# Cross-attention with a scan on one core: folded maxima, statistics on ScalarE, halved projections

## The chip, the cores and the metric

The kernel runs on one NeuronCore of a Trainium2 chip. The core has five engines with instruction queues of their own: TensorE (PE: matmuls and transposes, results into PSUM; its weight loads stand in the profile as PEld), VectorE (DVE), ScalarE (ACT), GpSimd (POOL) and SyncE (SP, which here issues nearly all DMAs). The metric is the time of one execution on the device, in microseconds. Before the change it was 2542.23 us, the median of three runs (2541.93 to 2543.82).

## The reference

One layer of a sequence model in fp32. Cut to what is computed:

```
x      = builder_state                                  # 4096 x 512
base   = layernorm(ctx, g1, beta1)                      # 3202 x 512
h      = x + mha(layernorm(x, g1, beta1), base)         # 8 heads of 64
U      = (layernorm(h, g2, beta2) @ W_in.T + b_in) @ Bmat   # 4096 x 64
s_t    = silu(s_(t-1) @ A.T) + U_t                      # a scan over 4096 steps
out    = h + states @ Cmat + mean(ctxb) @ W_prog.T + b_prog

mha:   scores = q @ k.T / 8;  softmax over 3202 keys;  @ v;  @ W_o.T + b_o
```

The softmax is over all 3202 keys of a query, with the row's maximum taken off first.

## The kernel before

**Preparation.** The context is read in 26 chunks of 124 or 123 keys (`keys`, `key0`, lines 44 to 49). Each is normalized (statistics on DVE, factors on POOL, scaling on ACT), transposed on PE and projected to values (`pv`, L505) and, four chunks at a time, to keys (`pk`, L531), which go out to DRAM (`vd`, `kd`). A side generator (`side`, L355) folds gains and biases into the weights between the chunks, and at its end `first_queries` (L284) normalizes the first 512 query rows and makes all four query tiles of block 0 (`heads`, L265: 4 head pairs, each two halves of 256 queries by four 128x256 matmuls into the PSUM tile `pq`, then one ACT eviction to `q`).

**Main part.** The work is 64 units: 8 query blocks of 512 by 4 head pairs by 2 halves of 256 queries. A unit takes 13 steps, one for each pair of key chunks. For step c:

- `scores` (PE, L576): four matmuls into `s`, a PSUM tile of [keys, head a, chunk b, 256 queries]; two such buffers.
- `keep` (ACT, L589): a copy of `s` to SBUF (`p`).
- `top` (DVE, `running`, L597): the running maximum over the steps, still one value per key row, head, chunk of the pair and query: 1024 elements.

After the 13th `top`, `spread` (PE, L605) transposes `top` in 128-query tiles: two tiles `tt` of four 124x124 blocks each; `maximum` (DVE, L615) reduces each to one value per head and query; `everywhere` (PE, L625) transposes these back over the key rows into `mb`. Then, again for each step: `subtract` (DVE, L633), `weights` (ACT, exp, L643), `add` (POOL, L651, the running sum `acc`) and `product` (PE, L660, into `po`). `finish` (L708) turns the sum into reciprocals (`both` POOL, `turn` and `back` PE, `inverse` DVE, `wide` ACT, `scale` DVE).

Beside the units run two kinds of other work, cut into pieces. `queries` (L788) prepares block Q+1: per 128 rows a load, the three pieces of `norm_pieces` (L767: `stats` on DVE, `factors` on POOL, `scaled` on ACT), a transposition and its copy; then four `heads` of 16 matmul records each, as one piece. `project` (L831) finishes block Q: per 128 rows a load, `row` (POOL), `outs` (PE, `pa`, four 128x512 matmuls in one piece), `x1` (DVE), `norm_pieces`, `mod` (POOL), a store, a transposition and copy, `inputs` (PE, `pu`) and `kept` (DVE, L900), which writes the scan's inputs `u`.

**Order.** Nothing in this part is in program order as written. `Plan` (L52) holds pieces with an engine, a cost in ns, what they come after, a due time, and the ring buffers they take and give back. `Plan.order` (L77) goes through a modelled time, picks for each free engine the ready piece with the smallest due time whose buffers fit, and the pieces are emitted in that order; each engine then executes its own in that order. On PE, entering a group of another kind costs `START`, staying in it `AGAIN`, and up to two pieces of the same kind are pulled together.

**End.** The last unit's row sums are partly made on PE (`last_sums`, L668), and the scan over the sequence follows, in blocks, with the output rows.

Of the kernel before, what the change touches and what calls it, by code (L numbers as in the profile page):

```python
# [20 lines left out]
P = 128  # L21
# [22 lines left out]
def keys(c):  # L44
    return CK if c < GC else CK - 1


def key0(c):
    return c * (CK - 1) + min(c, GC)


class Plan:  # L52
# [8 lines left out]
    START, AGAIN = 215, 90  # L61
# [6 lines left out]
    def add(self, name, engine, cost, run, after=(), due=0, take=(), give=(), kind=None):  # L68
        assert name not in self.pieces, name
        self.pieces[name] = dict(  # L70
# [6 lines left out]
    def order(self):  # L77
# [21 lines left out]
        while len(out) < len(pieces):  # L99
            for e in self.LATE:  # L100
# [3 lines left out]
                for p in ready[e]:  # L104
                    if fits(p):
                        more = p["kind"] and p["kind"] == last and run < 2
                        key = p["due"] - (6000 if more and e == "PE" else 0), p["at"]
                        if best is None or key < best[0]:
                            best = key, p
# [33 lines left out]
def xattn_ssm_kernel(  # L143
# [49 lines left out]
    bu = const.tile([P, 1], F32, name="bu")  # L193

# [70 lines left out]
    def heads(Q, hp, xns):  # L265

        pq = ps_m.tile([P, 512], F32, tag="m", name=f"pq_{Q}_{hp}")
        for half in range(2):
            for i in range(NC):
# [12 lines left out]
        qt[Q, hp] = t  # L282

    def first_queries(x0):  # L284
# [16 lines left out]
        for hp in range(NC):  # L301
            for _ in heads(0, hp, xns):
                yield
            yield

# [49 lines left out]
    def side():  # L355
# [62 lines left out]
        for k in (0, NS):  # L418
            nc.vector.tensor_copy(bu[k : k + NS], pb[:NS, 0:1])

# [170 lines left out]
    def running(w, c):  # L591

        n, s = keys(2 * c), w["ps"][c]
        before = w["s"][0] if c == 1 else w["top"]
        if c == 1:
            w["top"] = accp.tile([CK, 2, 2, QU], F32, tag="top", name=f"top_{w['name']}")
        nc.vector.tensor_tensor(w["top"][:n], s[:n], before[:n], ALU.max)  # L597

    def spread(w, t):

        tp = ps_m.tile([P, 2, 2, CK], F32, tag="m", name=f"tt_{w['name']}_{t}")
        w["tt", t] = tp
        for a in range(2):
            for b in range(2):
                nc.tensor.transpose(  # L605
                    tp[:, a, b, :],
                    w["top"][:, a, b, t * P : (t + 1) * P],
                    ident[:CK, :CK],
                )

    def maximum(w, t):

        if t == 0:
            w["m"] = small.tile([P, 2, 2], F32, tag="m", name=f"m_{w['name']}")
        nc.vector.tensor_reduce(  # L615
            w["m"][:, t, :], w["tt", t].rearrange("p a b k -> p a (b k)"), AX.X, ALU.max
        )
# [149 lines left out]
    def norm_pieces(plan, k, get, d, after, name, give):  # L767
# [3 lines left out]
        def stats_():  # L771
            v["mv"] = stats(get(), P, name)

        def factors_():
            v["fs"] = factors(v["mv"], P, name)

        def scaled_():
            v["xh"] = scaled(get(), v["fs"], P, name)
# [681 lines left out]
```

## Time and profile before

| | us |
|---|---|
| median of three runs | 2542.23 |
| the profiled execution | 2546.95 |
| its span, first to last instruction | 2545.1 |
| first scores matmul at | 262.67 |
| first `mb` (maxima of unit 0 spread) at | 291.42 |
| last `mb` at | 2441.61 |

The costliest groups of the page, with the number of instructions, the busy time and the mean of one:

| line, engine | what | count | busy us | mean ns |
|---|---|---|---|---|
| L651 POOL | `add` | 698 (and 64 first ones) | 1651.1 (152.2) | 2366 (2378) |
| L633 DVE | `subtract` | 832 | 997.9 | 1210 |
| L576 PE | `scores` | 6656 | 907.5 | 398 |
| L660 PE | `product` | 6656 | 880.1 | 391 |
| L643 ACT | `weights` | 832 | 876.4 | 1059 |
| L597 DVE | `top` | 704 (and 64 first ones) | 856.1 (78.0) | 1216 (1219) |
| L589 ACT | `keep` | 832 | 826.8 | 1006 |
| L270 PE | `heads` | 512 | 118.7 | 385 |
| L848 PE | `outs` | 240 | 110.4 | 603 |
| L615 DVE | `maximum` | 128 | 84.6 | 668 |
| L605 PE | `spread` | 512 | 73.8 | 278 |

Smaller rows of the answer by line: `bn_stats` L212 62 times on query and row tiles, 0.69 us each, `bn_aggr` L214 0.18; the POOL factors 0.22, 0.56 and 0.27 (L221, L223, L225); the scaling L233 on ACT 0.81; `kept` L900 on DVE 0.44; `x1` L858 on DVE 0.68; the PSUM copy `xn` on ACT 0.59.

How to read it: the busy time of a group is the union of its instructions' spans, and successive ones overlap, so counts times means are more than the busy time. A fp32 matmul stands as two records. What a piece costs its engine is best read from its start to the start of the next. An idle time is put down to what ended it last.

### The profile page before, as it was taken

The numbers are of one execution on the slowest core, as the hardware profiler recorded it, in microseconds if no ns is written. First come the engines' busy times: TensorE is split into PE (matmuls) and PEld (weight loads), VectorE is DVE, ScalarE is ACT, GpSimd is POOL, SyncE is SP. The second block draws the span as 40 slices with busy tenths as digits, with TensorE's granted clock in tenths as the row PEclk, the third lists the DMA queues.
The fourth block names the chain that finished last, engine by engine and source line by source line (L and its number), as shares of the span: only waits on it lengthen the run. The fifth ranks groups of instructions, "written<-read, shape, count | busy, mean of one in ns | idle before, by whom it ended". The sixth has DMA issues, their size and how long they took to land.

```text
span 2545.1 us, 44356 instructions
## 1 busy us (share of the span) xinstructions
PE 2439.3 (96%) x16648; PEld 1435.7 (56%) x16648; DVE 2128.5 (84%) x2322; ACT 1838.7 (72%) x2111; POOL 2071.1 (81%) x1195
## 2 busy tenths in 40 slices
PE   7989799999999999999999999999999999999997
PEld 3445455655565556655565556555665556555543
DVE  2220699999989999899989998999989998999974
ACT  2222688787878788787878887878878787878752
POOL 1010299899988999899989999899989998999973
PEclk9999999999999999999999999999999999999998
DMA  3422322112211221122211221222112221233364
GB/s 126 141 87 68 90 61 61 50 42 69 72 46 56 71 69 55 46 65 75 67 51 43 65 88 34 60 68 68 53 49 65 71 67 52 79 115 113 105 168 142
DMA packets 178035, 189.22 MB, mean 74 GB/s; under 512 B 14252, under 2 KB 151256, under 8 KB 177818
## 3 DMA queue, kind: packets, MB, share of 16 engines
q1 hardware_dynamic: 173270, 178.67, 23.5%
q10 hardware_dynamic: 4548, 7.67, 0.9%
q8 instruction: 134, 2.20, 0.4%
q14 instruction: 83, 0.68, 0.1%
HBM read 156.40 MB, written 29.89 MB: 73 GB/s over the span
## 4 chain that ended last, share of the span: by engine, by line
PE 52%; DVE 23%; issue 9%; ACT 6%; POOL 5%; DMA 3%; SPq 1%; ACTq 0%; POOLq 0%; DVEq 0%
PE s L576 16%; DVE top L597 14%; PE po L660 13%; DVE p L633 6%; POOL acc L651 5%; PE pq L270 4%; PE pa L848 4%; ACT p L589 3%; PE pv L505 3%; PE pk L531 3%; PE tt L605 2%; ACT p L643 2%; DMA x<-in_x_dram 2%; PE mb L625 1%; PE pu L894 1%
## 5 line engine op out<-in xcount | busy, mean ns | idle before, releaser
L651 POOL TENSOR_TENSOR acc<-p,acc 123x1024 f32<-123x1024 f32 x698 | 1651.1, 2366 | 65.3 <-ACT p L643 24.4
L633 DVE TENSOR_TENSOR p<-p,mb 123x1024 f32<-123x1024 f32 (+1 forms) x832 | 997.9, 1210 | 4.0 <-PE mb L625 3.8
L643 ACT ACTIVATE p<-p 123x1024 f32<-123x1024 f32 (+1 forms) x832 | 876.4, 1059 | 171.9 <-DVE p L633 169.2
L589 ACT COPY p<-s 123x1024 f32<-123x1024 f32 (+1 forms) x832 | 826.8, 1006 | 222.0 <-PE s L576 200.2
L576 PE MATMUL s<-q,k 64*123 64x256 f32 (+1 forms) x6656 | 907.5, 398 | 43.9 <-DVE top L597 31.9
L597 DVE TENSOR_TENSOR top<-s,top 123x1024 f32<-123x1024 f32 x704 | 856.1, 1216 | 53.1 <-ACT p L589 50.8
L660 PE MATMUL po<-p,v 123*64 123x256 f32 (+1 forms) x6656 | 880.1, 391 | 3.8 <-ACT p L643 2.7
L576 PEld LDWEIGHTS s<-q,k 64*123 64x123 f32 (+1 forms) x6656 | 574.3, 182 | 336.9 <-DVE top L597 152.1
L660 PEld LDWEIGHTS po<-p,v 123*64 123x64 f32 (+1 forms) x6656 | 416.7, 136 | 364.8 <-issue 154.8
L651 POOL TENSOR_TENSOR acc<-p,p 124x1024 f32<-124x1024 f32 x64 | 152.2, 2378 | 128.6 <-DMA k<-kd 77.6
L597 DVE TENSOR_TENSOR top<-s,p 124x1024 f32<-124x1024 f32 x64 | 78.0, 1219 | 60.3 <-DMA k<-kd 37.5
L221 POOL TENSOR_SCALAR ve_c<-mv_c 123x1 f32<-123x1 f32 (+1 forms) x26 | 5.8, 225 | 145.7 <-DVE mv_c L214 115.2
L270 PE MATMUL pq<-xn,wq 128*128 128x256 f32 x512 | 118.7, 385 | 0.0
L475 DVE COPY ct<-tp_c 128x492 f32<-128x492 f32 (+1 forms) x13 | 8.7, 671 | 127.2 <-PE tp_c L248 127.2
L848 PE MATMUL pa<-wo,o 128*128 128x512 f32 x240 | 110.4, 603 | 0.0
L270 PEld LDWEIGHTS pq<-xn,wq 128*128 128x128 f32 x512 | 94.8, 190 | 23.2 <-issue 9.4
L615 DVE TENSOR_REDUCE m<-tt 128x2 f32<-128x496 f32 x128 | 84.6, 668 | 22.0 <-PE tt L605 21.3
L539 ACT ACTIVATE ks<-pk,bias 128x492 f32<-128x492 f32 (+2 forms) x28 | 18.0, 642 | 111.5 <-PE pk L531 56.9
L505 PE MATMUL pv<-wv,ct 128*123 128x512 f32 (+1 forms) x208 | 97.2, 612 | 0.0
L531 PE MATMUL pk<-ct,wk 128*128 128x492 f32 (+2 forms) x224 | 89.2, 550 | 0.0
L716 POOL TENSOR_TENSOR both<-acc 124x512 f32<-124x512 f32 x63 | 80.8, 1283 | 2.4
L605 PE MATMUL tt<-ident,top 124*128 124x124 f32 x512 | 73.8, 278 | 9.0 <-DVE top L597 7.2
(182 smaller groups left out, 1331.9 us busy)
## 6 DMA issues: line engine op xcount, KB each, us to landing
k<-kd SPq DMA_DIRECT2D x396, 123.0 KB
v<-vd SPq DMA_DIRECT2D x396, 123.0 KB
k<-kd SPq DMA_DIRECT2D x72, 124.0 KB
v<-vd SPq DMA_DIRECT2D x72, 124.0 KB
xr<-in_x_dram SPq DMA_DIRECT2D x32, 256.0 KB
x1d<-xr SPq DMA_DIRECT2D x32, 256.0 KB
x<-in_x_dram SPq DMA_DIRECT2D x28, 256.0 KB
cx<-in_ctx_dram SPq DMA_DIRECT2D x22, 246.0 KB
```

Of the source, the lines that this page charges most:

```text
L270: nc.tensor.matmul(pq[:, half * QU : (half + 1) * QU], wq[:, i, hp * P : (hp + 1) * P], xns[half][:, i, :], start=(i == 0), stop=(i == NC ...
L505: nc.tensor.matmul(pv[:n, :H], ct[:, i, o : o + n], wv[:, i, :], start=(i == 0), stop=(i == NC - 1),)
L531: nc.tensor.matmul(pk[:, :n_g], wk[:, i, hp * P : (hp + 1) * P], ct[:, i, :n_g], start=(i == 0), stop=(i == NC - 1),)
L576: nc.tensor.matmul(s[:n, a, b, :], kts[(*w["at"][:2], c)][r, b * n : (b + 1) * n], q[r], start=True, stop=True,)
L589: nc.scalar.copy(t[:n], w["ps"][c][:n])
L597: nc.vector.tensor_tensor(w["top"][:n], s[:n], before[:n], ALU.max)
L605: nc.tensor.transpose(tp[:, a, b, :], w["top"][:, a, b, t * P : (t + 1) * P], ident[:CK, :CK],)
L633: nc.vector.tensor_tensor(t[:n], t[:n], w["mb"][:n].unsqueeze(2).to_broadcast([n, 2, 2, QU]), ALU.subtract,)
L643: nc.scalar.activation(t[:n], t[:n], AF.Exp)
L651: nc.gpsimd.tensor_tensor(w["acc"][:n], t[:n], before[:n], ALU.add)
L660: nc.tensor.matmul(w["po"][a * HD : (a + 1) * HD, 0, :], vts[(*w["at"][:2], c)][:n, b, a * HD : (a + 1) * HD], t[:n, a, b, :], start=(c == ...
L848: nc.tensor.matmul(v["pa"], o_t[Q, c, t // 2][:, t % 2 * P : (t % 2 + 1) * P], wo[:, c, :], start=(c == 0), stop=(c == NC - 1),)
```

## The change

Six edits. (1) The key chunks are cut so that the last pair has 124 rows. At the last step of a unit DVE folds the two chunks of the pair together: `s0 = max(s0, top0)` in PSUM, `top1 = max(s1, top1)`, `top0 = max(s0, top1)`, each of 512 elements, in place of one maximum of 1024. `spread` transposes only `top0`: four blocks into one tile, and `maximum` is one reduction. (2) In `norm_pieces` the two DVE statistics give way to two ACT passes with accumulated output, the negated mean (`mean`) and the sum of squares about it (`spread`); POOL makes the factors from them. (3) `kept` moves from DVE to ACT, with a doubled bias `bu2`. (4) `heads` and `outs` become two pieces each. (5) `first_queries` makes only head pair 0; pairs 1 to 3 become pieces of the plan, due 4 steps apart from step 4 on, and the first units wait for their own `q`. (6) The planner gets other entry costs, a penalty for a lone piece of a kind (`ALONE`) and a shift of due times by the sort of piece (`SHIFT`).

```diff
@@ keys, key0
 def keys(c):
-    return CK if c < GC else CK - 1
+    return {0: CK, 1: CK, 2: CK - 2, NDC - 1: CK}.get(c // 2, CK - 1)
 def key0(c):
-    return c * (CK - 1) + min(c, GC)
+    return sum(keys(k) for k in range(c))
@@ class Plan
-    START, AGAIN = 215, 90
+    START, AGAIN = 200, 65
+    RUN = 2
+    ALONE = dict(scores=600, product=2600)
+    SHIFT = {
+        "back": -2600, "both": -1300, "everywhere": -2600, "heads": 2000, "heads2": -5200,
+        "maximum": 18900, "output": -5200, "product": 1300, "query.spread": -5800,
+        "query.turn": 1200, "row.mean": 2000, "row.mod": 7800, "row.row": 1300, "row.spread": -600,
+        "row.turn": 2600, "spread": -2000, "turn": -1900, "weights": 1300,
+    }
...
+        due += self.SHIFT.get(sort, 0)
...
-                        more = p["kind"] and p["kind"] == last and run < 2
-                        key = p["due"] - (6000 if more and e == "PE" else 0), p["at"]
+                        due = p["due"]
+                        if p["kind"]:
+                            if p["kind"] == last and run < self.RUN:
+                                due -= 6000
+                            elif p["kind"] != last or run >= self.RUN:
+                                others = [o for o in ready[e] if o["kind"] == p["kind"] and o is not p]
+                                if not any(fits(dict(take=o["take"] + p["take"])) for o in others):
+                                    due += self.ALONE[p["kind"]]
@@ heads, first_queries
         for half in range(2):
+            if half:
+                yield
             for i in range(NC):
...
-        for hp in range(NC):
-            for _ in heads(0, hp, xns):
-                yield
+        first_xns.extend(xns)
+        pieces = heads(0, 0, xns)
+        next(pieces)
+        for _ in pieces:
             yield
+        yield
@@ side
             nc.vector.tensor_copy(bu[k : k + NS], pb[:NS, 0:1])
+            nc.vector.tensor_scalar(bu2[k : k + NS], pb[:NS, 0:1], 2.0, None, ALU.mult)
@@ running
+        if c == NDC - 1:
+            top0, top1 = (before[:n, :, b, :] for b in range(2))
+            nc.vector.tensor_tensor(s[:n, :, 0, :], s[:n, :, 0, :], top0, ALU.max)
+            nc.vector.tensor_tensor(top1, s[:n, :, 1, :], top1, ALU.max)
+            nc.vector.tensor_tensor(top0, s[:n, :, 0, :], top1, ALU.max)
+            return
@@ spread, maximum
-    def spread(w, t):
-        tp = ps_m.tile([P, 2, 2, CK], F32, tag="m", name=f"tt_{w['name']}_{t}")
-        w["tt", t] = tp
-        for a in range(2):
-            for b in range(2):
+    def spread(w):
+        tp = ps_m.tile([P, 2, 2, CK], F32, tag="m", name=f"tt_{w['name']}")
+        w["tt"] = tp
+        for t in range(2):
+            for a in range(2):
                 nc.tensor.transpose(
-                    tp[:, a, b, :],
-                    w["top"][:, a, b, t * P : (t + 1) * P],
-                    ident[:CK, :CK],
+                    tp[:, t, a, :], w["top"][:, a, 0, t * P : (t + 1) * P], ident[:CK, :CK]
                 )
-    def maximum(w, t):
-        if t == 0:
-            w["m"] = small.tile([P, 2, 2], F32, tag="m", name=f"m_{w['name']}")
-        nc.vector.tensor_reduce(
-            w["m"][:, t, :], w["tt", t].rearrange("p a b k -> p a (b k)"), AX.X, ALU.max
-        )
+    def maximum(w):
+        w["m"] = small.tile([P, 2, 2], F32, tag="m", name=f"m_{w['name']}")
+        nc.vector.tensor_reduce(w["m"], w["tt"], AX.X, ALU.max)
@@ norm_pieces
-        def stats_():
-            v["mv"] = stats(get(), P, name)
+        def mean_():
+            xh = v["xh"] = ln.tile([P, H], F32, tag="xh", name=f"xh_{name}")
+            v["nm"] = ln.tile([P, 1], F32, tag="nm", name=f"nm_{name}")
+            nc.scalar.activation(
+                xh, get(), AF.Copy, scale=-1.0 / H, accum_out=v["nm"]
+            )
+        def spread_():
+            v["sq"] = ln.tile([P, 1], F32, tag="sq", name=f"sq_{name}")
+            nc.scalar.activation(
+                v["xh"], get(), AF.Square, bias=v["nm"], accum_out=v["sq"]
+            )
         def factors_():
-            v["fs"] = factors(v["mv"], P, name)
+            rstd = v["rstd"] = ln.tile([P, 1], F32, tag="rstd", name=f"rstd_{name}")
+            nc.gpsimd.tensor_scalar(rstd, v["sq"], 1.0 / H, EPS, ALU.mult, ALU.add)
+            nc.gpsimd.tensor_tensor(rstd, rstd, neg_half, ALU.pow)
+            nc.gpsimd.tensor_tensor(v["nm"], v["nm"], rstd, ALU.mult)
...
-        plan.add((*k, "stats"), "DVE", 860, stats_, after, d, ["st", "mv"],
-                 [("st", (*k, "stats")), give])
...
+        plan.add((*k, "mean"), "ACT", 820, mean_, after, d, ["nm", "xh"])
+        plan.add((*k, "spread"), "ACT", 820, spread_, [(*k, "mean")], d + 1000, ["sq"])
@@ queries, head_pieces
+    def head_pieces(plan, Q, hps, xns, copied, d, apart, xn_):
+        for hp in hps:
...
+            plan.add(("heads", Q, hp), "PE", 1850, head, copied, d, ["m", "q"], xn_)
+            plan.add(("heads2", Q, hp), "PE", 1850, lambda v=v: next(v["heads"]),
+                     [("heads", Q, hp)], d + 1, [], xn_)
...
@@ project
-            def outs(v=v, r=r, t=t):
-                v["pa"] = ps_m.tile([P, H], F32, tag="m", name=f"pa_{r}")
-                for c in range(NC):
+            def outs(part, v=v, r=r, t=t):
+                if part == 0:
+                    v["pa"] = ps_m.tile([P, H], F32, tag="m", name=f"pa_{r}")
+                for c in (2 * part, 2 * part + 1):
...
+            plan.add((*k, "outs2"), "PE", 1850, partial(outs, 1), [(*k, "outs")], d + 1, [], o_)
...
             def kept(v=v, hs=hs, c0=c0):
-                nc.vector.tensor_scalar(
+                nc.scalar.activation(
                     u[hs, :, c0 : c0 + P // L].rearrange("s j c -> s c j"),
                     v["pu"][hs].rearrange("s (c j) -> s c j", j=L),
-                    bu[hs],
-                    2.0,
-                    ALU.add,
-                    ALU.mult,
+                    AF.Identity,
+                    bias=bu2[hs],
+                    scale=2.0,
                 )
...
-            plan.add((*k, "kept"), "DVE", 420, kept, [(*k, "inputs")], d + 8 * STEP, [],
+            plan.add((*k, "kept"), "ACT", 260, kept, [(*k, "inputs")], d + 8 * STEP, [],
@@ unit
-            q = [("q", Q, hp)] if Q else []
+            q = [("q", Q, hp)] if Q or hp else []
...
-                plan.add(("top", i, c), "DVE", 1145, partial(running, w, c),
+                plan.add(("top", i, c), "DVE", 1145 if c < NDC - 1 else 2000, partial(running, w, c),
...
+        plan.add(("spread", i), "PE", 530, partial(spread, w), [("top", i, NDC - 1)], d, ["m"],
+                 [("top", ("top", i, 1))])
+        plan.add(("maximum", i), "DVE", 665, partial(maximum, w), [("spread", i)], d + 1000,
+                 ["max"], [("m", ("spread", i))])
@@ the plan
-            dict(q=[("heads", 0, hp) for hp in range(NC)]),
+            dict(q=[("heads", 0, 0)], xn=[("first", half) for half in range(2)]),
         )
+        head_pieces(plan, 0, range(1, NC), first_xns, [], 4 * STEP, 4 * STEP,
+                    [("xn", ("first", half)) for half in range(2)])
```

## The prediction

> **What bounds the kernel now.** I read the shares of the engines first, then the span cut at four points that mean something in the code: the first scores matmul (262.67 us), the first `mb` (the maxima of unit 0, 291.42), the last `mb` (unit 63, 2441.61) and the end.
>
> ```profile
> PE 2439.3 (96%) x16648; PEld 1435.7 (56%) x16648; DVE 2128.5 (84%) x2322; ACT 1838.7 (72%) x2111; POOL 2071.1 (81%) x1195
> ...
> 0.00:262.67 262.67, 233.56 (x706) 115.63 (x707) 46.41 (x107) 66.62 (x106) 33.33 (x99) 0.99 0.33 106
> 262.67:291.42 28.75, 20.08 (x136) 12.88 (x137) 15.95 (x14) 14.92 (x15) 0.00 (x0) 0.94 0.38 114
> 291.42:2441.61 2150.19, 2102.22 (x15370) 1263.90 (x15368) 2011.97 (x2067) 1721.78 (x1905) 1989.91 (x1051) 1.00 0.22 65
> 2441.61:2545.10 103.49, 83.48 (x440) 43.25 (x438) 54.19 (x134) 35.43 (x86) 47.88 (x46) 0.93 0.57 168
> ```
>
> The windows rows give the length, then busy time of PE, PEld, DVE, ACT, POOL. The main stretch is 84% of the span, and in it PE is idle for 48 of 2150 us, DVE for 138, POOL for 160, ACT for 428. So PE sets the pace, and a microsecond of PE work is worth a microsecond. What little PE idles is, in the waits of that stretch, almost all one thing:
>
> ```profile
> PE s L576 <- DVE top L597: 24.8, 56, 1.2
> PE tt L605 <- DVE top L597: 6.8, 6, 1.6
> PE po L660 <- ACT p L643: 2.7, 8, 1.2
> ```
>
> The scores have two PSUM buffers; one comes free when `keep` (ACT) and `top` (DVE) have read it. Last, the price of a PE group, read from one group's start to the next group's:
>
> ```profile
> 211.30 3.62 PE L270 MATMUL pq<-xn,wq 128*128 128x256 f32 x16
> 214.76 3.60 PE L505 MATMUL pv<-wv,ct 128*123 128x512 f32 x8
> ...
> 269.52 1.13 PE L576 MATMUL s<-q,k 64*123 64x256 f32 x8 [0.90 <-DVE top L597]
> 271.00 1.13 PE L576 MATMUL s<-q,k 64*123 64x256 f32 x8 [0.35 <-DVE top L597]
> 273.02 1.13 PE L576 MATMUL s<-q,k 64*123 64x256 f32 x8 [0.89 <-DVE top L597]
> ...
> 834.84 1.08 PE L660 MATMUL po<-p,v 124*64 124x256 f32 x8
> 835.86 0.64 PE L722 MATMUL pd<-ident,both 124*128 124x124 f32 x4
> 836.43 1.13 PE L576 MATMUL s<-q,k 64*123 64x256 f32 x8
> 837.49 1.08 PE L660 MATMUL po<-p,v 124*64 124x256 f32 x8
> ...
> 843.02 3.70 PE L848 MATMUL pa<-wo,o 128*128 128x512 f32 x8
> 846.65 1.99 PE L576 MATMUL s<-q,k 64*123 64x256 f32 x16
> 848.58 1.73 PE L660 MATMUL po<-p,v 123*64 123x256 f32 x14
> ```
>
> One step of scores costs 1.06 us, two in a row 1.93: 0.87 a step and 0.20 for entering the group. A product step costs 1.02, two in a row 1.88 in the median of the trace: 0.86 and 0.15. A block of four transposes costs 0.57, two blocks in a row 1.00: 0.42 and 0.15. A whole `pq` or `pa` costs 3.65 and 3.63. Summing these prices over the groups of the main stretch gives 2086 us; the other 64 of its 2150 are the 48 idle and groups held up inside. I call them lost time.
>
> **The change, part by part.** Group counts are from the built instruction order of both kernels, main stretch (first to last `mb`).
>
> *Folded maxima, PE.* 126 transpose blocks in 91 groups become 63 in 63: 126 x 0.42 + 91 x 0.15 = 66.9, now 63 x 0.57 = 36.0, so -30.9 us.
>
> *Halved projections and the new order, PE.* 28 `pq` and 30 `pa` each get a second entry, with other groups between the halves: 58 x 0.15 = +8.7. Score groups go from 667 to 679 (+2.4), product groups from 698 to 673 (-3.8), one product moves behind the last `mb` (-0.9), one `py` before it (+1.0). With the transposes: **-23.4 us of PE work**.
>
> *Heads 1 to 3 of block 0, out of the preparation.* A `pq` there costs 3.46 (211.30 to 214.76), and PE has no idle time from 204 to 260, so -10.4. No DMA is issued by them; the load and store order on SP stays, and on ACT their three evictions (0.69 each) go from among the `ks`/`vs` copies to among the first `keep`s. Their time covered the normalization of the last context chunk: about 3 us (statistics 0.87, factors 1.05 and gaps, scaling 0.81) between two chunk steps of 3.86 each, still covered. Bounds: -10.4, or -7 if a `ks` store is then late (such a wait cost ACT up to 14.9 us once, at an earlier group).
>
> *The same heads beside the first steps.* There two steps take 3.50 us (269.52 to 273.02), PE waiting 1.25 of them for DVE. The order is now two scores, one half head: 1.93 + 1.90 = 3.83. Six times 0.33 is +2.0, and the k transfer that holds the second scores until 265.02 hides some: +1.5 to the first `mb`. Bounds 0 and +11.4 (nothing hidden).
>
> *DVE.* The last `top` of a unit (1.13 from start to start) becomes three operations of 512 elements. Nearest row: `x` L858, 128x512 from PSUM, 0.68 long, 0.61 from start to start; three and a dependent start make 1.9. The first writes into PSUM, which no row shows; 0.53 (half of 1.13) and 1.13 bound each. One `maximum` less saves 0.59: near zero per unit. Statistics leave: 58 tiles x 0.82 (0.69 + 0.18, overlapped) = -47.6; `kept`: 30 x 0.28 = -8.3. DVE sheds some 50 of its 2012 us. Directly that is worth nothing, as DVE isn't the bound; it makes `top` less late. Against it, the last scores buffer of each unit is held 0.8 longer: behind it on DVE wait the subtractions and on PE the next scores; at worst 63 x 0.8 = 50 us, at best nothing because products stand between. I take nothing.
>
> *ACT.* Two passes per tile, mean and squares, with an accumulated output that no row has. Nearest: `COPY xn` 128x512, 0.59, and the scaling L233 with two per-partition operands, 0.81. The Trainium skill, "ScalarE: Activation LUTs" (What ACT_TABLE_LOAD costs), gives 186 ns + 0.833 per element and 93 for a pointer operand: an estimate of 0.61 and 0.71, which fits both rows. I take 0.72 each: 58 x 1.44 = 83 us, and `kept` 30 x 0.28 (as the 128-element tanh L1032) = 8. ACT then has 1813 of about 2120.
>
> *Two rules speak against this part.* The row for the first: PE waits 31.6 us for DVE and 3.4 for ACT, and ACT idles 428 us. The same page (Rules for kernel authors) puts add and multiply on VectorE, not ScalarE. By the rule the tile goes from 0.82 us to 1.44, 36 us of engine time lost over 58 tiles; by the rows the time leaves the engine PE waits for. PE's bound decides: I charge nothing. The row for the second: the trace has a single ACT_TABLE_LOAD, 1.28 us at 7.54. The same page (Table sets) counts a load of 1283 ns and a drain, 2.66 us, at each switch of set, and its list for the exp set does not name Square; if Square lay elsewhere, 58 x 2 switches would add 309 us to ACT. The new kernel's built order holds one load, at the start. So nothing.
>
> *POOL.* Three small operations a tile as before; the last is now a product of two columns, 0.27 (the row L225) to 0.57 (the pow L223): 0 to +17 us, covered. It matters as a floor: 750 adds that follow one another at 2.43 (1822), `both` 82, `row` and `mod` 78, factors 70, together 2052 us in the main stretch.
>
> *Tail.* After the last `mb` PE needed 26.4 us to the scan (2441.61 to 2468.03). The row sums now stand between the products, which wait for the weights at 1.13 a step. Priced as above: 25.8, so -0.6; bounds -4 and +2.
>
> *Lost time.* 64 us now. If DVE's relief removed all 31.6 us of waiting it would be 32; if the added ACT work came in front of `keep` it would grow. The two pull on the same loop (scores, keep, top), DVE's -50 against ACT's +91 where ACT has three times the idle time. I take -8.
>
> **Sum:** -10.4 + 1.5 - 23.4 - 0.6 - 8 = -40.9. The profiled execution took 2546.95 (span 2545.1), so 2506.0; the median of the three runs, 2542.23, stands 4.7 lower: **2501 us**.
>
> **Rivals.** *Lost time goes with the relief:* shorter PE blocks and a lighter DVE take away over half of it, say 37. For it: the waits are of one kind. Against: POOL's floor of 2052 then nearly binds, since PE work alone is 2063. 2542.2 - 32.9 - 37 = 2472. *Half given back:* the first `top`s and folds come late, and lost time grows by 21: 2530. For it: DVE `top` already waits 68 us for `keep` in this stretch. *Slower: ACT takes DVE's place in the scores loop.* A mean or square pass of 0.72 in front of a `keep` delays `top` and the next scores by as much; with two buffers PE can't run ahead. Of the 83 us added, 33 landing on PE (40%) eat the whole gain; at 60%, 50 us, the time is 2542.2 - 32.9 + 50 = 2559. Against it: ACT's idle time, and that products can be run meanwhile.
>
> **Chances.** Forecast, own range 2485 to 2522: 0.62. Lost time gone: 0.13. Half given back: 0.13. Within 0.2% (5 us, about what a measurement tells from no change): 0.03. Slower: 0.09. The range 2477 to 2530 leaves out most of the slower case and the best part of the second.
>
> **What would show it.** Right: `tt` in 64 groups of 0.57; first scores near 252; six half `pq` between the scores and first `mb` some 30 us later; main stretch near 2119; DVE busy there 50 less, ACT 90 more. Wrong: `s <- DVE top` or `DVE top <- ACT p` grown by tens of us; a second table load; preparation shorter by less than 7; half `pq` above 1.9.

## The result and the profile after

| | before | after |
|---|---|---|
| median of 4 runs, us | 2543.03 (2541.93 to 2544.24) | 2513.53 (2512.27 to 2515.3) |
| the profiled execution | 2546.95 | 2515.3 |
| its span | 2545.1 | 2513.5 |
| first `pq` of block 0 | 204.0 | 209.9 |
| first scores | 262.67 | 257.90 |
| first `mb` | 291.42 | 291.02 |
| last `mb` | 2441.61 | 2410.80 |

The ratio of the times is 0.9884, with a 95% interval of 0.9867 to 0.9902: 29.5 us less. The first part of the page, busy time and instructions by engine:

```profile
PE 2418.6 (96%) x16390; PEld 1409.1 (56%) x16392; DVE 2087.6 (83%) x2242; ACT 1922.3 (76%) x2373; POOL 2066.7 (82%) x1195
```

The same four windows as before the change (length, then busy PE, PEld, DVE, ACT, POOL, granted clock, DMA share, GB/s):

```profile
0.00:257.90 257.90, 225.51 (x659) 107.17 (x659) 46.82 (x109) 64.70 (x103) 33.78 (x99) 0.98 0.35 108
257.90:291.02 33.12, 30.71 (x180) 22.06 (x180) 16.78 (x16) 16.86 (x18) 0.00 (x0) 0.91 0.35 104
291.02:2410.80 2119.78, 2080.02 (x15115) 1235.70 (x15114) 1969.98 (x1984) 1805.53 (x2166) 1988.96 (x1053) 1.00 0.22 66
2410.80:2513.50 102.70, 82.32 (x441) 44.13 (x441) 54.05 (x134) 35.22 (x86) 44.01 (x44) 0.92 0.57 168
```

Row by row against before: preparation 4.8 us shorter, unit 0 longer by 4.4, main stretch shorter by 30.4, tail by 0.8. Nearly everything is won in the main stretch, and the first two rows cancel. In the main stretch DVE is busy 42 us less, ACT 84 more. PE's work by the group prices is 2064.1, so lost time is 2119.8 - 2064.1 = 55.7. The waits of PE there (engine, line, what ended the wait; us in total, times, longest):

```profile
PE s L605 <- DVE top L633: 15.0, 47, 1.5
PE pd L753 <- POOL both L747: 7.2, 19, 0.6
PE po L691 <- ACT p L674: 4.7, 5, 1.5
PE tt L641 <- DVE top L629: 3.2, 13, 0.8
```

The two waits for `top` fell from 31.6 to 18.2; the waits for `both` and for the weights grew by some 6. PE is not the only one that waits. ACT's `keep` writes into a buffer of `p`, and a buffer comes free when `add` (POOL) and `product` have read it. The waits of `keep` that an `add` ended, before the change and after it (both from 292 to 2410 us):

```profile
ACT p L589 <- POOL acc L651: 3.4, 3, 2.1
...
ACT p L618 <- POOL acc L682: 27.7, 18, 2.5
```

Before the change two other operations of POOL ended another 11 us of them, so POOL's part went from 14 to 28.

The new pieces, in DVE's timeline at the end of a unit (start, duration, operation):

```profile
848.22 0.69 DVE L627 TENSOR_TENSOR s<-s,top 124x512 f32<-124x512 f32 x1
848.94 0.69 DVE L628 TENSOR_TENSOR top<-s,top 124x512 f32<-124x512 f32 x1
849.67 0.69 DVE L629 TENSOR_TENSOR top<-s,top 124x512 f32<-124x512 f32 x1
850.27 2.34 DVE L664 TENSOR_TENSOR p<-p,mb 123x1024 f32<-123x1024 f32 x2
852.53 0.67 DVE L648 TENSOR_REDUCE m<-tt 128x4 f32<-128x496 f32 x1
```

From the first start to the subtraction behind, the three operations of the fold take 2.05 us. The one that writes into PSUM is as long as the others. And ACT's two statistics passes:

```profile
840.32 0.62 ACT L805 ACTIVATE xh_y<-x 128x512 f32<-128x512 f32 x1
840.84 0.19 ACT L805 ACTIVATION_READ_ACCUMULATOR xh_y<-x 128x1 f32 x1
...
842.42 0.73 ACT L811 ACTIVATE xh_y<-x,nm_y 128x512 f32<-128x512 f32 x1
843.04 0.19 ACT L811 ACTIVATION_READ_ACCUMULATOR xh_y<-x,nm_y 128x1 f32 x1
843.13 1.04 ACT L674 ACTIVATE p<-p 123x1024 f32<-123x1024 f32 x1
```

Each accumulated output brings a second instruction that reads the accumulator. Where something follows at once, the mean pass takes 0.63 us from its start to the next start and the squares 0.72 (medians over 35 and 43 of the 58 tiles). In the rows above the mean pass is followed by an idle time, the squares by an exp at 843.13.

### The profile page after: what moved, and what is told of

The parts are those of the page before. It is cut to its first block, busy times and chain, and to the rows that moved or that the text cites. A ratio compares the mean times of both kernels' runs of the same rounds, so it can differ in the third digit from the quotient of the medians.

```text
span 2513.5 us, 43994 instructions
## 1 busy us (share of the span) xinstructions
PE 2418.6 (96%) x16390; PEld 1409.1 (56%) x16392; DVE 2087.6 (83%) x2242; ACT 1922.3 (76%) x2373; POOL 2066.7 (82%) x1195
## 4 chain that ended last, share of the span: by engine, by line
PE 38%; DVE 22%; POOL 17%; issue 13%; ACT 6%; DMA 2%; SPq 1%; ACTq 0%; POOLq 0%; DVEq 0%
POOL acc L682 15%; DVE top L633 12%; PE s L605 12%; PE po L691 9%; DVE p L664 6%; ACT p L618 3%; PE pv L534 3%; PE pk L560 3%; PE pq L294 3%; PE pa L900 2%; ACT p L674 2%; PE tt L641 1%; POOL both L747 1%; PE pd L753 1%; DMA cx<-in_ctx_dram 1%
## 5 line engine op out<-in xcount | busy, mean ns | idle before, releaser
L682 POOL TENSOR_TENSOR acc<-p,acc 122x1024 f32<-122x1024 f32 (+1 forms) x698 | 1653.0, 2368 | 60.7 <-ACT p L674 17.9
L664 DVE TENSOR_TENSOR p<-p,mb 123x1024 f32<-123x1024 f32 (+2 forms) x832 | 991.7, 1208 | 23.2 <-PE mb L656 23.2
L674 ACT ACTIVATE p<-p 123x1024 f32<-123x1024 f32 (+2 forms) x832 | 875.4, 1058 | 138.9 <-DVE p L664 134.2
L618 ACT COPY p<-s 123x1024 f32<-123x1024 f32 (+2 forms) x832 | 829.6, 1006 | 168.4 <-PE s L605 121.6
L605 PE MATMUL s<-q,k 64*123 64x256 f32 (+2 forms) x6656 | 911.1, 398 | 25.2 <-DVE top L633 15.0
L691 PE MATMUL po<-p,v 123*64 123x256 f32 (+2 forms) x6656 | 877.5, 390 | 6.6 <-ACT p L674 4.7
L633 DVE TENSOR_TENSOR top<-s,top 123x1024 f32<-123x1024 f32 (+1 forms) x640 | 777.3, 1215 | 11.5 <-ACT p L618 9.3
L605 PEld LDWEIGHTS s<-q,k 64*123 64x123 f32 (+2 forms) x6656 | 574.9, 182 | 337.7 <-DVE top L633 115.9
L691 PEld LDWEIGHTS po<-p,v 123*64 123x64 f32 (+2 forms) x6656 | 423.5, 136 | 357.9 <-issue 145.5
L294 PE MATMUL pq<-xn,wq 128*128 128x256 f32 x512 | 126.7, 390 | 0.0
L294 PEld LDWEIGHTS pq<-xn,wq 128*128 128x128 f32 x512 | 92.2, 189 | 31.6 <-issue 21.2
L568 ACT ACTIVATE ks<-pk,bias 128x492 f32<-128x492 f32 (+3 forms) x28 | 18.0, 643 | 118.6 <-PE pk L560 58.4
L534 PE MATMUL pv<-wv,ct 128*123 128x512 f32 (+2 forms) x208 | 99.0, 621 | 0.0
L747 POOL TENSOR_TENSOR both<-acc 124x512 f32<-124x512 f32 x63 | 80.8, 1283 | 3.0
```

The costliest lines, as they stand in the source:

```text
L294: nc.tensor.matmul(pq[:, half * QU : (half + 1) * QU], wq[:, i, hp * P : (hp + 1) * P], xns[half][:, i, :], start=(i == 0), stop=(i == NC ...
L534: nc.tensor.matmul(pv[:n, :H], ct[:, i, o : o + n], wv[:, i, :], start=(i == 0), stop=(i == NC - 1),)
L605: nc.tensor.matmul(s[:n, a, b, :], kts[(*w["at"][:2], c)][r, b * n : (b + 1) * n], q[r], start=True, stop=True,)
L618: nc.scalar.copy(t[:n], w["ps"][c][:n])
L664: nc.vector.tensor_tensor(t[:n], t[:n], w["mb"][:n].unsqueeze(2).to_broadcast([n, 2, 2, QU]), ALU.subtract,)
L674: nc.scalar.activation(t[:n], t[:n], AF.Exp)
```

## The experiments

Two theories. **Theory 1**: PE's work by the group prices sets the time, and each edit is worth the PE work it takes away. **Theory 2**: the order, and which engine has slack in it, sets the time; edits don't add. "Main" is the main stretch, "lost" is main minus PE's work by the group prices, and "PE work" is worked out from group counts and prices, not measured. The kernels were timed in groups of four, each group beside the kernel before: from "after, again" on, its median is 2543.93 for the first four rows, 2545.56 for the next four and 2544.25 for the last four. The times in us compare within a group, the ratios in the whole table.

| kernel | us | ratio, 95% interval | PE work | DVE busy | main | lost | first `pq` | first scores |
|---|---|---|---|---|---|---|---|---|
| before (profile) | | | 2087.5 | 2012.0 | 2150.2 | 62.7 | 204.0 | 262.7 |
| after (profile) | 2513.53 | 0.9884 [0.9867, 0.9902] | 2064.1 | 1970.0 | 2119.8 | 55.7 | 209.9 | 257.9 |
| after, again | 2515.22 | 0.9883 [0.9868, 0.9898] | 2064.1 | 1971.2 | 2122.4 | 58.3 | 210.3 | 258.3 |
| before + planner | 2537.15 | 0.9973 [0.9961, 0.9984] | 2083.3 | 2013.1 | 2139.8 | 56.5 | 204.4 | 263.1 |
| after, old planner | 2545.87 | 1.0007 [0.9998, 1.0016] | 2052.7 | 1972.2 | 2148.6 | 95.9 | 209.9 | 257.9 |
| before + chunk sizes | 2551.38 | 1.0030 [1.0018, 1.0042] | 2087.5 | 2011.9 | 2148.6 | 61.1 | 208.9 | 267.6 |
| after, DVE statistics | 2553.96 | 1.0034 [1.0021, 1.0046] | 2071.0 | 2025.7 | 2160.5 | 89.5 | 210.6 | 258.6 |
| after, no fold | 2552.60 | 1.0025 [1.0015, 1.0035] | 2096.8 | 1957.9 | 2156.9 | 60.2 | 212.2 | 260.1 |
| after, whole projections | 2559.00 | 1.0055 [1.0041, 1.0069] | 2040.4 | 1972.9 | 2162.1 | 121.7 | 211.2 | 259.2 |
| after, heads in preparation | 2522.07 | 0.9907 [0.9891, 0.9922] | 2064.1 | 1971.6 | 2121.7 | 57.6 | 211.7 | 270.1 |
| after, small pair moved | 2509.95 | 0.9866 [0.9851, 0.9881] | 2064.1 | 1971.0 | 2122.3 | 58.2 | 206.5 | 254.5 |
| before + fold | 2575.98 | 1.0128 [1.0112, 1.0143] | 2061.2 | 2029.4 | 2172.4 | 111.3 | 209.8 | 268.5 |
| before + ACT statistics | 2557.47 | 1.0048 [1.0034, 1.0061] | 2086.5 | 1961.3 | 2160.0 | 73.5 | 205.1 | 263.7 |
| before + halves | 2556.18 | 1.0049 [1.0035, 1.0062] | 2084.2 | 2009.4 | 2158.4 | 74.2 | 202.6 | 261.3 |

### The changed kernel again

The same kernel, timed together with the next three.

> The changed kernel once more, to see what repeats. Both theories: 2513 us, ratio to before 0.988. The question is the preparation: in the first profile the first scores matmul started at 257.9, 4.8 us earlier than before where three head projections of 3.46 (10.4) had left. If the missing 5.6 us come from late transfers of that one execution, it starts near 252 here; if they belong to the kernel, near 258 again.

The gain repeats, and so does the late start: first scores at 258.3, so the missing 5.6 us of the preparation belong to the kernel and not to one execution. Its profile differs from the first one by 2.6 us in the main stretch and by less than 1 elsewhere, which is the scatter to allow for in the columns above.

### The planner alone, and the work alone

The first takes the kernel before and only the planner's numbers and rule; the second takes the changed kernel and puts the old ones back.

```diff
 class Plan  (before + planner)
-    START, AGAIN = 215, 90
+    START, AGAIN = 200, 65
+    RUN = 2
+    ALONE = dict(scores=600, product=2600)
+    SHIFT = {
...
@@ after, old planner: the same lines the other way round
```

> The kernel before with the changed planner alone (entry costs, ALONE, SHIFT). Theory 1, PE's work sets the time: by group counts the PE work of the main stretch falls from 2087.5 to 2083.3 us, so 4 us faster than before, 2539. Theory 2, the order and the waits set it: the lost time falls and most of the gain comes from here, 15 us or more, 2528 or less.

> The changed kernel with the planner's constants of before (no ALONE, no SHIFT, entry costs 215 and 90). Theory 1: its PE work in the main stretch is 2052.7 us against 2064.1, so at equal lost time 11 us faster than the changed kernel, 2502. Theory 2: without the shifts the added ACT passes and the later folds come at bad times, the lost time grows by 15 to 30 us, 2528 to 2543.

The planner alone gives 6.8 us: more than the 4 of Theory 1, far from the 15 of Theory 2. Of the 10.4 us that its main stretch is shorter, 4.2 are PE's work and 6.2 lost time. The work alone gives nothing: 1.0007, though its PE work is the lower of the two (2052.7, since the old planner makes fewer and longer runs of one kind). Its lost time is 95.9, 40 more than the changed kernel's, where Theory 2 had 15 to 30. In its main stretch PE's longest wait is

```profile
PE s L586 <- DVE top L614: 40.1, 79, 1.5
```

and DVE, which PE waits for, itself waits:

```profile
DVE top L614 <- ACT p L599: 80.6, 69, 2.3
DVE m L629 <- PE tt L622: 51.8, 37, 2.7
DVE s L608 <- ACT p L599: 32.4, 21, 2.4
```

The first and third line are `top` and the fold waiting for `keep`: 113 us together. In the changed kernel, where the new planner orders the same pieces, these are

```profile
DVE top L633 <- ACT p L618: 68.5, 60, 2.4
...
DVE s L627 <- ACT p L618: 8.8, 11, 1.7
```

77 together, and before the change

```profile
DVE top L597 <- ACT p L589: 68.0, 64, 4.1
```

So under the old planner the added ACT work does stand in front of `keep`, as the slower rival had it, and the new planner takes it out of there. Theory 1 falls here: 35 us less PE work than before, and the same time.

### The chunk sizes alone

```diff
 def keys(c):
-    return CK if c < GC else CK - 1
+    return {0: CK, 1: CK, 2: CK - 2, NDC - 1: CK}.get(c // 2, CK - 1)
...
```

> The kernel before with the new chunk sizes alone (124 rows in the last pair, 122 in the third). If the sizes delay the preparation: first scores some 6 us later than 262.7, 2549 in all. If not: 262.7 and 2543, the same as before.

Slower by 7 us, and the main stretch is not what got longer: the first `pq` comes at 208.9 instead of 204.0. It stays late by 5 to 8 us in every kernel with these sizes and the small pair third. I come back to it at the moved pair.

### One part taken back at a time

Statistics and `kept` on DVE; two `tt` and the 1024-element `top` at the last step; `pq` and `pa` as one piece each. All under the new planner and its due times, with the new chunk sizes.

```diff
@@ norm_pieces, kept  (DVE statistics)
-        plan.add((*k, "mean"), "ACT", 820, mean_, after, d, ["nm", "xh"])
-        plan.add((*k, "spread"), "ACT", 820, spread_, [(*k, "mean")], d + 1000, ["sq"])
...
+        plan.add((*k, "stats"), "DVE", 860, stats_, after, d, ["st", "mv"],
+                 [("st", (*k, "stats")), give])
@@ running  (no fold)
-        if c == NDC - 1:
...
@@ head_pieces, project  (whole projections)
-            plan.add(("heads", Q, hp), "PE", 1850, head, copied, d, ["m", "q"], xn_)
-            plan.add(("heads2", Q, hp), "PE", 1850, lambda v=v: next(v["heads"]),
+            plan.add(("heads", Q, hp), "PE", 3700, head, copied, d, ["m", "q"], xn_)
```

> The changed kernel with the statistics and kept back on DVE. Theory 1, PE's work sets the time: PE work 2071.0 against 2064.1 us (its order has more groups), so 7 us slower than the changed kernel, 2520. Theory 2, DVE's relief pays: top comes late again and lost time grows, 15 us or more slower, 2529 or more. If the ACT passes cost something: faster than 2513.

> The changed kernel with the maxima unfolded: 8 blocks transposed a unit, two reductions, one last top of 1024. Theory 1: PE work 2096.8 against 2064.1, 33 us slower than the changed kernel, 2546. Theory 2, the folds' longer hold of a scores buffer gives part of it back: less than 20 us slower, under 2533.

> The changed kernel with heads and outs as whole pieces, priced 3700 in the planner. Theory 1: fewer entries, PE work 2040.4 against 2064.1, so 24 us faster than the changed kernel, 2490. Theory 2: a block of 3.65 us on PE starves the loop of scores, keep and top, lost time grows by as much or more, 2513 or slower.

All three are slower than the kernel before the change, by 7 to 13 us, and by the ratios some 36 to 44 us slower than the changed kernel. PE's work explains the missing fold (2096.8 instead of 2064.1, 33 of its 36 us, lost time nearly the same) and neither of the others: 2071.0 and 2040.4 come with lost times of 89.5 and 121.7. With whole projections PE waits as follows:

```profile
PE s L601 <- DVE top L629: 42.4, 89, 1.2
PE po L687 <- ACT p L670: 10.8, 18, 1.4
```

With the statistics on DVE:

```profile
PE tt L641 <- DVE top L629: 18.9, 11, 3.8
PE s L605 <- DVE top L633: 18.1, 48, 1.5
```

The first line grew most: PE waits for the last operation of the fold, 18.9 us against 3.2. DVE is then busy 2025.7 us of 2160.5 and idle for 135. A reservation belongs to all three: the due times were set for the full change, so what is measured is the part together with an order that no longer fits it, not the price of the part. The shifts of the pieces `mean`, the statistics' `spread` and `heads2`, for instance, fall away with those pieces.

### One part alone

The complement: each part on the kernel before, under the old planner.

> The kernel before with the new chunk sizes and the folded maxima alone, under its own entry costs and due times. PE's work in the main stretch falls from 2087.5 to 2061.2 by the group prices. Theory 1, PE's work sets the time: 2543 - 26 + 7 (the sizes in the preparation) = 2524, lost time as before (63). Theory 2, the pieces pay only in an order that fits them: the fold holds the last scores buffer of a unit 0.8 us longer in every unit and nothing is moved out of its way; lost time up by 20 to 35, time 2545 or more, and s<-DVE top grown in PE's waits.

> The kernel before with the statistics and kept on ScalarE alone. PE's work 2086.5 (-1). DVE loses about 50 us of work, ScalarE gains about 85. Theory 1: 2542; if VectorE's load was what made top late, lost time falls by 10 to 20 and the time to 2525 to 2532. Theory 2: ScalarE's passes stand in front of keep in an order that isn't made for them; lost time up by 15 to 30, time 2555 to 2570, DVE top<-ACT p grown.

> The kernel before with heads and outs in two pieces each, nothing else. PE's work 2084.2 by the group prices (-3: the added entries are paid back by fewer groups of scores). Theory 1: 2540. If the 3.6 us blocks were what starved the scores loop, lost time falls by 10 to 20 and the time to 2520 to 2530. Theory 2, the old due times don't fit: 2550 or more.

Each alone is a loss. The same reservation holds: the old due times were set for the kernel without these parts, and no run sets them anew for one part. **The fold** (with the sizes it needs) costs 31.7 us although PE's work falls by 26.3. That is more than either theory had (2524, or 2545 and more). The main stretch is 22.2 longer, with DVE busy for 17.4 more in it; the preparation is longer by 5.8 and unit 0 by 1.5. PE's waits in the main stretch are

```profile
PE s L578 <- DVE top L606: 35.8, 73, 1.8
PE po L664 <- ACT p L647: 9.0, 18, 1.4
```

and DVE's timeline ahead of one of the 0.5 us waits of scores (it ended at 550.17):

```profile
546.64 1.22 DVE L606 TENSOR_TENSOR top<-s,top 123x1024 f32<-123x1024 f32 x1
547.77 1.21 DVE L637 TENSOR_TENSOR p<-p,mb 123x1024 f32<-123x1024 f32 x1
548.90 1.22 DVE L606 TENSOR_TENSOR top<-s,top 123x1024 f32<-123x1024 f32 x1
550.03 1.21 DVE L637 TENSOR_TENSOR p<-p,mb 123x1024 f32<-123x1024 f32 x1
```

No row has an idle time in brackets: each operation starts where the last one ends, `top` and `subtract` 1.13 us apart, and this has been so since 534.22, at the start of the unit. A step's `top` and `subtract` take 2.26 us of DVE, and its scores and product at most 2.08 of PE (1.06 + 1.02). In this unit DVE is full and PE runs into it. Over the whole stretch DVE still idles 143 us: 36 before the first `top` of a unit, 51 before later ones, where it waits for `keep`, and the rest before other operations, most of them at the turns between units. The waits of scores don't stand where the folded buffer is held, either: of the 57 us that PE idles before scores, none is before the second step of a unit, which needs that buffer, and 53 are before steps 3 to 5 and 8 to 12 (counted from 0).

**The statistics on ACT** (with `kept`) cost 13.2 alone. DVE is lighter by 51 us, and idle for 199 instead of 138; but `top` now waits for `keep`:

```profile
DVE top L599 <- ACT p L591: 106.6, 106, 2.8
DVE m L617 <- PE tt L607: 57.1, 42, 3.6
```

106.6 against 68.0 before. **The halves** cost 11.9 alone; their lost time is 74.2, with PE's wait for `both` up from 2.7 to 10.3 and DVE's for `tt` from 20.6 to 45.3. Why the finer pieces delay just these two was not separated.

By medians: planner -6.8, fold +31.7, statistics +13.2, halves +11.9, and the heads' exit about -6 (next section). They add up to +44, and together they measure -29.5. Theory 2 holds in its main point: the parts repair each other. The kernel with all the work and the old planner splits the repair: without the planner the sum is +51 (with the heads' exit as measured under the new one), and this kernel measures +2. So some 49 us come from the parts of the work among themselves; and the planner, worth 6.8 on the old work, is worth 31 on the new. How they do it is read from the waits and was not tried by itself: the fold needs DVE time, which the statistics give; the statistics need ACT passes kept off `keep`, which the new planner does.

### Heads of block 0 back in the preparation

```diff
-        pieces = heads(0, 0, xns)
-        next(pieces)
-        for _ in pieces:
-            yield
+        for hp in range(NC):
+            pieces = heads(0, hp, xns)
...
-        head_pieces(plan, 0, range(1, NC), first_xns, [], 4 * STEP, 4 * STEP,
```

> The changed kernel with the heads 1 to 3 of block 0 back in the preparation. By the prediction's terms 8.9 us slower than the changed kernel (10.4 in the preparation, 1.5 back in unit 0), 2522; by the first profile of the changed kernel, where unit 0 took 33.1 us against 28.75, 10.4 - 4.4 = 6 slower, 2519.

0.9907 against 0.9883 for the changed kernel: moving the heads out is worth about 6 us (0.0024 x 2544; the intervals overlap a little). The two first windows of this kernel show both sides of it:

```profile
0.00:270.14 270.14, 236.85 (x707) 116.72 (x707) 46.65 (x109) 66.67 (x106) 33.80 (x99) 0.98 0.33 103
270.14:297.16 27.02, 18.25 (x133) 11.29 (x133) 16.22 (x15) 14.92 (x15) 0.00 (x0) 1.00 0.38 115
```

From first `pq` to first scores it takes 58.4 us, and 48.0 in the changed kernel: the move takes 10.4 out of the preparation. Unit 0 then takes 33.1 instead of 27.0, so it gives 6.1 back (5.3 against the second profile). By the trace some 4 to 5 us remain, by the ratios 6; the prediction's terms made it 8.9.

### The small pair moved

The pair of chunks with 122 keys becomes the twelfth.

```diff
-    return {0: CK, 1: CK, 2: CK - 2, NDC - 1: CK}.get(c // 2, CK - 1)
+    return {0: CK, 1: CK, NDC - 2: CK - 2, NDC - 1: CK}.get(c // 2, CK - 1)
```

> The changed kernel with one size moved: the pair of chunks with 122 keys is the twelfth instead of the third, so that the chunks from the third pair on start two rows earlier. The new sizes alone made the first pq 5 us late (208.9 us against 204.0), and nothing in PE's list of work explains it. If the small pair stands in the way of the early loads and stores (SP's context loads of 8 to 10 us instead of 6 to 7, the kd store that the eviction ks waits for): first pq near 204, first scores near 252, and 2508, some 6 us under the changed kernel (2513.5). If it is the changed last pair, or any other start row, that does it: first pq stays at 209 to 210 and the time at 2514. The main stretch is 2120 in both cases.

First `pq` 206.5, first scores 254.5, and 2509.95 us: somewhat over half of what was expected if the small pair did it all (204 and 252). It has the lowest median, 34 us under before. Against the changed kernel the intervals of the ratios overlap; in the traces its first scores come 3.4 and 3.8 us earlier than in the changed kernel's two profiles, and its main stretch (2122.3) lies between theirs. What the size does is seen on SP's queue of transfers. Before the change (start, time that the issue took, transfer):

```profile
15.47 6.35 SPq L461 DMA_DIRECT2D cx<-in_ctx_dram  x4
...
26.22 7.56 SPq L461 DMA_DIRECT2D cx<-in_ctx_dram  x1
```

After it:

```profile
15.86 9.79 SPq L490 DMA_DIRECT2D cx<-in_ctx_dram  x4
...
29.00 8.79 SPq L490 DMA_DIRECT2D cx<-in_ctx_dram  x1
```

With the small pair moved:

```profile
15.72 6.03 SPq L490 DMA_DIRECT2D cx<-in_ctx_dram  x4
...
25.39 8.50 SPq L490 DMA_DIRECT2D cx<-in_ctx_dram  x1
```

The four loads at 15 us are chunks 4 to 7, of which the change makes two 122 rows long. The semaphore writes that follow the issue of a load, read from the trace:

```
load                     issued   semaphore written at
before, chunk 0, 124 rows   0.72   five times, last at  7.47
before, chunk 4, 123 rows  15.47  15.90  23.23 23.25 23.79
after,  chunk 4, 122 rows  15.86  16.27  25.50 25.99
```

The first write stands 0.4 to 0.5 us behind the issue. The others are the DMA engines that finish: four for 124 rows, three for 123, two for 122. The Trainium skill, "DMA: Bandwidth & Descriptors" (Why a DMA increments its semaphore by 16 and not by 1), says that the number of engines is the largest up to 16 that divides the outer dimension on both sides: 4, 3 and 2 here. The trace agrees. A load on two engines lands 10.1 us after its issue instead of 8.3, everything behind it on SP is later, and in the changed kernel PE runs dry at a place where it did not before. Before the change and after it:

```profile
104.40 0.58 PE L248 MATMUL tp_c<-ident,xh_c 123*128 123x123 f32 x4
104.83 3.60 PE L505 MATMUL pv<-wv,ct 128*123 128x512 f32 x8
...
110.29 1.08 PE L270 MATMUL tp_c<-ident,xh_c 123*128 123x123 f32 x4 [5.74 <-ACT xh_c L255]
111.23 5.36 PE L534 MATMUL pv<-wv,ct 128*123 128x512 f32 x8
```

With the pair moved that transposition starts at 103.58, without a wait. The remaining 2.5 us of the moved pair arise later, between 143 and 187 us, where PE's clock is granted at half for 10.2 us against 3.4 before; what leads to that was not separated.

## Why the prediction was right, and where it was not

The forecast was 2501, with an own range of 2485 to 2522 inside the wider one of 2477 to 2530; the median is 2513.53. Against the profiled execution the working gave a span of about 2504 and it is 2513.5. By its own terms:

| term | taken | measured |
|---|---|---|
| preparation | -10.4 | -4.8 |
| unit 0 | +1.5 | +4.4 |
| PE's work, main stretch | -23.4 | -23.4 by the same prices (PE's busy time: -22.2) |
| lost time | -8 (64 to 56) | -7 (62.7 to 55.7) |
| main stretch in all | -31.4 | -30.4 |
| tail | -0.6 | -0.8 |

The 9 us by which the sum is off lie in the first two rows (5.6 and 2.9) and 1 in the main stretch. The row of PE's work is no measurement, since it comes from the same counts and prices; the busy time beside it is one.

**Mis-sized: the preparation.** The heads are worth what was taken for them (10.4, from the kernel that puts them back). What is missing is a term: the chunk sizes were priced with the fold and not as transfers. The sum said that "the load and store order on SP stays", which is true and not enough: the loads got slower, and the first `pq` came 5.9 later. The row for it was in the old trace, 124-row loads with five semaphore writes and 123-row ones with four.

**Mis-sized: unit 0.** The heads were taken as +1.5 here; against the kernel that puts them back (27.0, itself 1.7 less than before the change) they cost unit 0 6.1 us. The 3.83 us for a pair of steps with a half head is right; the turn of the unit was not priced. PE's timeline:

```profile
261.51 1.99 PE L294 MATMUL pq<-xn,wq 128*128 128x256 f32 x8
263.43 1.99 PE L605 MATMUL s<-q,k 64*122 64x256 f32 x16
...
287.43 0.62 PE L641 MATMUL tt<-ident,top 124*128 124x124 f32 x4 [2.41 <-DVE top L629]
287.98 3.12 PE L605 MATMUL s<-q,k 64*124 64x256 f32 x16
291.02 1.11 PE L656 MATMUL mb<-ident,m 128*124 128x128 f32 x4
```

Half a `pq` takes 1.92, a pair of steps with it 3.84 (261.51 to 265.35, the next `pq`). But before `tt` PE waits 2.41 us for the fold, which nothing covers in unit 0, and in this execution the scores behind run on half a clock: 3.12 instead of 1.99. In the second profile of the same kernel they took 1.99, and unit 0 took 32.3. The bound of +11.4 held.

**Right, for a reason that fell: the main stretch.** "A microsecond of PE work is worth a microsecond" gave the right number and isn't a rule of this kernel. The other term, -8 of lost time, was chosen between two pulls and not derived; that -7 came of it is luck in part, since 13 us less waiting for `top` stand against some 6 more for `both` and the weights. And the new planner, which the prediction priced by group counts alone, decides whether there is a gain at all (1.0007 without it). Three kernels have less PE work than the changed one (2052.7, 2040.4 and 2061.2) and are no faster than before; the last of them, the fold alone, takes 26 us of PE work away and loses 32.

The sentence on DVE's relief falls with it: "Directly that is worth nothing, as DVE isn't the bound". With the fold and without the relief DVE is busy 2026 to 2029 us, and both such kernels have main stretches of 2160 to 2172. In the kernels measured the main stretch was never shorter than PE's work plus 55.7, nor than DVE's busy time plus 126.7. Before the change it stood near both of these floors at once, 7 and 12 us above them; the view that hid this was the busy share over the stretch, in which DVE's idle time at the turns of the units looks like slack inside them. That DVE's load is what makes these two slow is read from the traces (DVE without a gap in the unit shown); it was not tried by itself, for instance by a longer operation on DVE alone. For the old planner with all the work, and for the whole projections, the main stretch is 40 and more above both floors. For the first of them the cause is the order: the same pieces under the new planner give 29 us. Whether its entry costs, its penalty or its due times do it stays open, and so does the cause for the whole projections.

**Not in this account: POOL.** The rival with the lost time gone named POOL's floor, 2052 us by its prices, as what would then nearly bind. The changed kernel has come nearer to that floor. `keep` waits 28 us for POOL instead of 14, and in the chain of work that ended last, on the page, the adds have 15% of the span after the change and 5% before. POOL's work is the same in all kernels (busy 1983 to 1998 us in the main stretch), so no run here shows whether it sets part of the 55.7 us that remain.

**The smaller steps.** `tt` in single groups of 0.57, `pq` halves of 1.92 (taken 1.90) and no second table load: as forecast. (The 1283 ns and 2.66 us that the prediction gives for a load stand on the page it names under What ACT_TABLE_LOAD costs; the list is under Table sets.) ACT's passes were taken at 0.72 each and cost 0.63 and 0.72; its load grew by 84 (taken 91). DVE fell by 42 (taken 50). The prediction's own terms make 45, since the 0.18 us a unit that it calls near zero is 11 us over 63 units; and with the fold at 2.05 per unit instead of 1.9, some 10 us, they make 35. So 7 us of the relief are not accounted for. POOL's last factor takes 0.19, under both bounds (0.27 and 0.57), and POOL's busy time stayed, 1989. The fold's hold of the scores buffer was bounded at 50 us and taken at nothing: in the main stretch the scores that need this buffer waited 2.1 us in all.

**The rivals.** Slower by ACT in front of `keep` was given 0.09 and is a real mechanism: it shows in the old order (106.6 and 113 us of waiting for `keep`) and not in the new one (77 against 68 before). What was argued against it, ACT's idle time, holds in both orders and is not what decides; by these waits it is where the passes stand in ACT's queue. Lost time gone did not come: it fell by 7 of the 37 that this rival had.

## What to carry to other kernels

When two engines are both busy for most of a stretch (here 98 and 94%), price an edit against both, inside the repeated part and not over the stretch: here a step cost DVE 2.26 us and PE 2.08, and the average hid it. Parts of a retuned change are not worth what they measure one at a time: three of these were losses when added alone and losses again when taken out. And a row count in a tile is also a transfer size: before changing one, read how many DMA engines finish such a load.

## What the runs showed of the hardware

- The number of DMA engines that end a load fell from 4 to 3 to 2 as its rows went from 124 to 123 to 122, and the landing from 8.3 to 10.1 us for the last step.
- A PE idle time of a few microseconds can be paid twice. After the 5.74 us before 110.29 the projection behind took 5.20 us from start to start (111.23 to 116.43), where the same one took 3.43 before the change (104.83 to 108.26), and after the 2.41 before `tt` the granted clock was 0.59 from 288 to 292. It is not always so. An idle time of 2.10 us that ended at 381.5 was followed by the full clock in this profile; in the second profile of the same kernel the same 2.10 us ended at 381.9, the clock was half from 382.9 to 386.3, and a step of scores took 2.07 instead of 1.13. In these traces the half clock comes in pieces of 3.41 us, of twice that or, once, of four times that (before + planner, from 264.8), but for the scan at the end; here from 288.7 to 292.1. The Trainium skill, "TensorE: Matmul & The Clock Gate" (Part 1: The HAM clock gate), has a window of this length.
- A maximum of 512 elements a row on DVE takes 0.69 us whether it writes into PSUM or into SBUF.
- An accumulated output on ACT brings a second instruction of 0.19 us. It overlaps its neighbours: from its start to the start of the instruction behind the read, the Copy pass, 0.63 long, takes 0.63 us, and the Square pass, 0.72 long, takes 0.72.
